# Two graph-attention layers on 64 graphs: rows of exponentials turned in VectorE's 32x32 squares and written in 128-byte pieces, and each output stored right behind its last addition

## The chip, the cores and the metric

The kernel runs on one core of a Trainium2 chip. The metric is the device time of one execution in microseconds. Three executions took 3341.45, 3341.65 and 3340.55 us; the median is 3341.45 us.

## The reference

There are 64 independent graphs of N = 256 nodes with D = 512 features, and a 0/1 adjacency matrix for each. Each graph goes through two residual layers, and everything is float32.

```python
# layer 0: GAT with two attention stages
h = maximum(layernorm(x), 0)
#   stage 1: 4 heads of 256, softmax over sources, concat, bias, elu
#   stage 2: 1 head of 512, softmax over sources, bias
x = x + gat(adj, h, W1, ..., W2, ...)
# layer 1: attention with 8 heads of 64, softmax over neighbours, relu
h = maximum(layernorm(x), 0)
x = x + attend(h, adj, W_proj, W_att, b_att)

# in each stage, for every head:
e    = leaky_relu(a_src[i] + a_dst[j], 0.2)
e    = where(mask, e, -big)
attn = softmax(e)
out  = attn @ xl
```

The kernel avoids the exponential of a 256x256 matrix per head. exp(leaky_relu(s + d)) is the larger of exp(s)exp(d) and exp(0.2 s)exp(0.2 d). Divided by exp(d), which cancels in the softmax, it is the larger of exp(s) and exp(0.2 s) times exp(-0.8 d). So only three vectors of exponentials are needed for a head: two that lie along partitions (one number for each row), and one, exp(-0.8 d), that must lie along the free dimension and be the same on all 128 partitions. Bringing that last vector from "one number per partition" to "a row on every partition" is what most of the change is about.

## The kernel before, in words

A graph's 256 nodes are T = 2 tiles of P = 128 partitions; a node's number is t*128 + q. The three attention stages are called 1, 2 and 3. Every graph goes through steps named as methods of `Graph`: `load`, `stats1` and `norm1` (layer norm), `away1` and `turn1` (the transpose of the normed features, by way of DRAM), the products `m1a`, `m1b` (with W1), `m2` (W2) and `m3` (W_proj), each of them made of seven part products `p1` to `p7` and `c22` with TensorE, `kept` copies on ScalarE (L60) and additions on VectorE (L253), then `exp1`, `edges1`, `gat1`, `out1`, `elu1` for stage 1, and the same with 2 and 3.

In `exp1`, `exp2` and `exp3` ScalarE computes the three exponentials (L275, L466) into a small tile `exs`, which is taken anew for each graph. `spread` (L230) then brings the third one to rows: a DMA on ScalarE's queue writes it to DRAM as `kept` (L233), in pieces of T floats, 8 bytes, since a partition holds the T values of a head side by side; then DMAs on SyncE's queue read it back, broadcast to all partitions (L238): tiles `bc` of two heads, 2 KB in one piece for each partition, 256 KB in all (1 KB and 128 KB in stage 2, which has one head). The row comes back with t innermost, so ScalarE reads every second float of it. `weigh` (L277) makes one 128x256 block of unnormalised attention: ScalarE multiplies the row by a number of each partition (L280, tile `wy`), VectorE takes the maximum with another number and applies the mask (L281, tile `e`). `gat1` (L382), `gat2` (L434) and `gat3` (L484) multiply by `e` on TensorE; the matmuls also give the sums of the softmax, and `out1` (L390, L392), `out2` and `out3` (L490, L492) divide. `out3` ends with GpSimd's addition to the residual `x2` (L494), and `store` (L501) writes `x2` to the output by SyncE's queue. `range` (L497, L498) takes the largest and smallest exponential of a graph, which at the very end decides whether a general path has to run; with these inputs it does not.

The order of work is written out by hand. The kernel's recording mode is a manual schedule: each engine runs its instructions, and each queue issues its DMAs, in the order in which the steps are called. `head`, `order` and `tail` are strings of steps; `run` calls `order` once for each r from 1 to 63, and a step's first number says which graph it is for, relative to r. So one round of `order` works on up to four graphs at once: stages of graph r+1's first products, graph r's stages 1 and 2, graph r-1's stages 2 and 3, and graph r-2's end of stage 3. Of `order` the places that matter here are

```
... 0 edges1 0, 0 edges1 1, 0 m1b p4, ..., 0 gat1 0 0, ...   (graph r, start of a round)
... -2 out3 1 1, -2 out3 1 0, 0 out1 0 1, ...                (last addition to graph r-2)
... 0 exp2, 1 m1a p6, -2 store, -1 edges3 0, ...             (its store)
... 1 m1a p4, 1 m1b p2, 1 exp1, -1 edges3 6, 1 m1b p6, ...   (end of a round)
```

`exp1` stands at the end of a round, and its rows are first used at the start of the next one.

Buffers: four `bc` tiles of two heads (one of stage 2), three `wy`, nine `e`, four banks of PSUM (`pm`) that the products and all `gat` steps share.

Of the kernel before, what the change touches and what calls it, by code (L numbers as in the profile page):

```python
# [17 lines left out]
P = 128  # L18
SLOPE = 0.2
# [78 lines left out]
def short_path(ctx, tc, flags, x, adj, w1, att_src1, att_dst1, b1, w2, att_src2, att_dst2, b2, w_proj, w_att,  # L98
               b_att, out):

    nc = tc.nc
    B, N, D = x.shape
    H1, F1 = att_src1.shape
    HF = H1 * F1
    D2 = w2.shape[1]
    H3 = w_att.shape[0]
    K3 = w_att.shape[1] // 2
    T = N // P
    DC = D // P
    HC = HF // P  # L110
    G = 4
# [26 lines left out]

    ends = const.tile([P, 2, B], F32, name="ends")

    L1, L2, L3 = 4, 1, 2 * G
# [84 lines left out]

    def spread(w, heads):  # L230

        kept = dram.tile([heads, P, T], F32, name=f"kept{heads}")
        nc.scalar.dma_start(kept.rearrange("h p t -> p h t"), w)  # L233
        rows = []
        for h in range(0, heads, 2):
            k = min(2, heads)
            bc = work.tile([P, k, P, T], F32, name=f"bc{k}", bufs=3 * k - 2)
            nc.sync.dma_start(bc.rearrange("p h q t -> p (h q t)"), rows_of(kept[h:h + k], k * N))  # L238
            rows += [bc[:, i].rearrange("p q t -> p t q") for i in range(k)]
        return rows  # L240

    def spread_at_once(w, heads, h):

        pm = ps_mm.tile([P, 512], F32, name="pm")
        for t in range(T):
            nc.tensor.matmul(pm[:, t * P:(t + 1) * P], w[:, h, t:t + 1].to_broadcast([P, P]), ident, start=True, stop=True)
        return pm[:, :N].rearrange("p (t q) -> p t q", t=T)

    def total(dst, pm, add):
        if add is None:  # L250
# [18 lines left out]
        total(lg3[:, t, half, :], pm[:, :L3], add if add is None else add[:, :L3])  # L269
        total(xl3[:, t, half * G:(half + 1) * G, :K3], heads(pm), add if add is None else heads(add))  # L270

    def exps(ex, n, a, o):

        for i, of, by in ((2, o, SLOPE - 1.0), (0, a, 1.0), (1, a, SLOPE)):
            nc.scalar.activation(ex(slice(i * n, (i + 1) * n)), of, AF.Exp, scale=by)  # L275

    def weigh(dst, bc, xw, yw, mask, op):  # L277

        wy = work.tile([P, T, P], F32, name="wy", bufs=3)
        nc.scalar.activation(wy, bc, AF.Copy, scale=yw)  # L280
        nc.vector.scalar_tensor_tensor(dst, wy.rearrange("p t q -> p (t q)"), xw, mask, ALU.max, op)  # L281

    class Graph:

# [29 lines left out]
        def stats1(self):  # L314
            n = Norm()
            for t in range(T):
                n.part(self.xs, t)
            self.ro = n.end()

            exs = self.exs = small.tile([P, 6 * (H1 + 1 + H3)], F32, name="exs")  # L320
            self.ex1 = exs[:, :6 * H1].rearrange("p (i t) -> p i t", t=T)
            self.ex2 = exs[:, 6 * H1:6 * (H1 + 1)].rearrange("p (i t) -> p i t", t=T)
            self.ex3 = exs[:, 6 * (H1 + 1):].rearrange("p (i h t) -> p i h t", i=3, t=T)

        def norm1(self):
            self.h = norm(self.xs, *self.ro)
# [37 lines left out]


        def exp1(self):
            exps(lambda sl: self.ex1[:, sl].rearrange("p h t -> p t h"), H1, xl1[:, :, 0, :L1], xl1[:, :, 1, :L1])
            self.bc1 = spread(self.ex1[:, 2 * H1:], H1)
            self.zt = [work.tile([P, HF], F32, name=f"z{t}", bufs=1) for t in range(T)]

        def edges1(self, h):
            e = self.e[1, h] = work.tile([P, T, N], F32, name="e", bufs=9)
# [40 lines left out]
                left(self.a2, HC // 2)  # L413

        def exp2(self):
            exps(lambda sl: self.ex2[:, sl].rearrange("p h t -> p t h"), 1, xl2[:, :, 0, :L2], xl2[:, :, 1, :L2])
            self.bc2 = None if self.b == B - 1 else spread(self.ex2[:, 2:3], 1)

        def edges2(self):
            e = self.e[2] = work.tile([P, T, N], F32, name="e", bufs=9)  # L420
            bc = self.bc2[0] if self.bc2 else spread_at_once(self.ex2[:, 2:3], 1, 0)
            for s in range(T):
                weigh(e[:, s, :], bc, self.ex2[:, 0, s:s + 1], self.ex2[:, 1, s:s + 1],
                      self.mask[:, s, :], ALU.mult)
# [36 lines left out]
        def exp3(self):  # L461
            nc.vector.tensor_tensor(lg3[:, :, :, :G], lg3[:, :, :, :G],
                                    batt_sb.rearrange("p (a h) -> p a h", a=2)[:, None].to_broadcast([P, T, 2, G]),
                                    ALU.add)
            for i, at, by in ((2, G, SLOPE - 1.0), (0, 0, 1.0), (1, 0, SLOPE)):
                nc.scalar.activation(self.ex3[:, i].rearrange("p (a h) t -> p t a h", a=2), lg3[:, :, :, at:at + G],  # L466
                                     AF.Exp, scale=by)
            self.bc3 = None if self.b == B - 1 else spread(self.ex3[:, 2], H3)

        def edges3(self, h):  # L470
            e = self.e[3, h] = work.tile([P, T, N], F32, name="e", bufs=9)
            bc = self.bc3[h] if self.bc3 else spread_at_once(self.ex3[:, 2], H3, h)
            for s in range(T):
                weigh(e[:, s, :], bc, self.ex3[:, 0, h, s:s + 1], self.ex3[:, 1, h, s:s + 1],
                      self.cap[:, s, :], ALU.min)
# [74 lines left out]
    class Weights:  # L550
# [56 lines left out]
        sums2 0, w sums2 1, 0 exp1, w sums2 2, 0 caps, w sums2 3, 0 edges1 1, 0 edges1 0, 0 edges1 3, 0  # L607
        cap3, 0 edges1 2, 0 gat1 0 0, 0 out1 0 0, 0 gat1 0 1, 0 out1 0 1, 0 gat1 1 0, 0 elu1 0 0, 0 out1 1
        0, 0 elu1 0 1, w load3, 0 gat1 1 1, 1 load, 0 out1 1 1, w dots3 7, 1 stats1, 0 turn2 0 0, 0 elu1 1
        0, 1 masks, 0 turn2 0 1, 0 elu1 1 1, 1 norm1, w dots3 1, 0 m2 p1, w dots3 2, w dots3 0, w dots3 6, 1  # L610
        away1, 0 turn2 1 0, 0 turn2 1 1, w dots3 5, w dots3 4, w dots3 3, 1 turn1, 0 m2 p6, w sums3 0, 0 m2
        p2, w sums3 1, w sums3 2, 0 m2 p7, 0 m2 p4, 0 m2 p5, 1 m1a p1, 1 m1a p6, 0 m2 c22, 1 m1a p5, 0 m2
        p3, 0 exp2, 1 m1a p7, 1 m1a c22, 1 m1b p1, w sums3 3, 1 m1a p4, 1 m1a p3, 1 m1a p2, 1 exp1, 1 bias,
        1 m1b p6, 1 m1b p2, 1 m1b p5, 1 caps
    """
    order = """
        -2 edges3 7, -2 gat3 0 0, -2 edges3 5, -2 gat3 0 1, -1 edges2, 0 m1b p7, -2 out3 0 1, -2 out3 0 0,
        -1 gat2 0, 0 m1b c22, -1 out2 0, -1 stats3 0, 0 m1b p3, -1 gat2 1, 0 edges1 0, 0 edges1 1, 0 m1b p4,
        -1 out2 1, 0 cap3, 1 load, 0 gat1 0 0, 0 edges1 2, 0 edges1 3, 0 out1 0 0, -2 gat3 1 1, -2 gat3 1 0,
        -1 stats3 1, 0 gat1 0 1, -1 norm3, -2 out3 1 1, -2 out3 1 0, 0 out1 0 1, 0 elu1 0 0, 0 elu1 0 1, 0  # L620
        gat1 1 0, -1 turn3, 0 out1 1 0, 0 gat1 1 1, 0 out1 1 1, 1 stats1, -1 m3 p1, 0 turn2 0 0, 0 turn2 0
        1, 0 elu1 1 1, 0 elu1 1 0, -1 m3 p2, -1 m3 p5, 1 masks, 1 norm1, -1 m3 p6, 0 m2 p1, 0 turn2 1 0, 0
        turn2 1 1, 1 away1, -1 m3 p7, 1 bias, -1 m3 c22, 0 m2 p2, -1 m3 p4, -2 range, -1 m3 p3, -1 exp3, 1
        turn1, 0 m2 p6, 0 m2 p5, 0 m2 p7, 1 caps, 1 m1a p1, 0 m2 c22, 0 m2 p3, 0 m2 p4, 0 exp2, 1 m1a p6, -2
        store, -1 edges3 0, -1 edges3 1, 1 m1b p1, 1 m1a p7, 1 m1a p5, 1 m1a c22, -1 edges3 2, 1 m1a p2, -1
        edges3 4, 1 m1a p3, -1 edges3 3, 1 m1a p4, 1 m1b p2, 1 exp1, -1 edges3 6, 1 m1b p6, 1 m1b p5
    """
    tail = """
        -2 range, 0 m1b p5, 0 m1a p2, -1 edges2, -2 gat3 0 0, 0 m1a c22, 0 m1b p6, -2 gat3 0 1, -2 out3 0 1,
        0 m1b p2, -2 edges3 5, -1 gat2 0, 0 exp1, 0 m1a p4, -1 out2 0, -1 stats3 0, -2 edges3 7, -1 gat2 1,  # L630
        -2 gat3 1 0, -1 out2 1, -1 stats3 1, -1 norm3, -2 out3 0 0, -2 gat3 1 1, -2 out3 1 1, -1 turn3, -1
        m3 p1, -1 m3 p2, -1 m3 p5, -1 m3 p6, -1 m3 p7, -1 m3 c22, -2 out3 1 0, -1 m3 p4, -1 m3 p3, -1 exp3,
        -1 range, -1 edges3 1, -1 edges3 4, -1 edges3 0, -1 edges3 3, -1 edges3 2, -1 edges3 5, -1 edges3 7,
        -1 edges3 6, -1 gat3 0 0, -1 gat3 0 1, -2 store, -1 gat3 1 1, -1 out3 0 1, -1 out3 1 1, -1 gat3 1 0,
        -1 out3 0 0, -1 out3 1 0, -1 store
    """
    weights = Weights()

# [293 lines left out]
```

## Time and profile before

| | |
|---|---|
| median of three timed executions | 3341.45 us |
| profiled execution | 3281.43 us |
| its span, first to last instruction | 3279.7 us |
| mean granted TensorE clock | 0.993 |
| TensorE matmul busy | 3155.8 us (96%) |
| VectorE, ScalarE, GpSimd busy | 2267.6, 1959.6, 1178.3 us |
| DMA | 279.19 MB, mean 85 GB/s |
| `wy`, L280, 1646 x | 524 ns each, 746.9 us |
| ScalarE waiting for `bc` ahead of it | 199.4 us in 54 waits |

The profiled execution is one execution, recorded by the hardware's profiler, and here it is 60 us shorter than the timed ones. A row "A <- B: total, times, longest" in a list of waits says that engine A stood idle ahead of the named work until B was done. In a timeline a line gives the start in us from the beginning of the span, the duration, the engine or its queue ("SPq", "ACTq"), the line of the kernel, the operation, and how many are merged; for a DMA the duration is that of its issue, not of the transfer.

### The profile page before, as it was taken

The numbers are of one execution on the slowest core, as the hardware profiler recorded it, in microseconds if no ns is written. First come the engines' busy times: TensorE is split into PE (matmuls) and PEld (weight loads), VectorE is DVE, ScalarE is ACT, GpSimd is POOL, SyncE is SP. The second block draws the span as 40 slices with busy tenths as digits, with TensorE's granted clock in tenths as the row PEclk, the third lists the DMA queues.
The fourth block names the chain that finished last, engine by engine and source line by source line (L and its number), as shares of the span: only waits on it lengthen the run. The fifth ranks groups of instructions, "written<-read, shape, count | busy, mean of one in ns | idle before, by whom it ended". The sixth has DMA issues, their size and how long they took to land. (4 is left out here: it accounts for less than half of the span.)

```text
span 3279.7 us, 60652 instructions
## 1 busy us (share of the span) xinstructions
PE 3155.8 (96%) x21808; PEld 2663.1 (81%) x21808; DVE 2267.6 (69%) x6189; ACT 1959.6 (60%) x4867; POOL 1178.3 (36%) x1433
## 2 busy tenths in 40 slices
PE   4999999999999999999999999999999999999997
PEld 3788888888888888888888888888888888888886
DVE  7667667667667677676676676676776766766765
ACT  2566566566556566655665565566566556665654
POOL 3243343343343342332433433423333334334332
PEclk8999999999999999999999999999999999999998
DMA  4222333323323333323223223233333233332231
GB/s 140 65 79 83 88 87 85 88 88 78 94 82 84 88 82 91 86 83 89 80 82 91 87 79 88 82 91 86 83 91 86 82 89 81 78 94 87 79 94 34
DMA packets 350751, 279.19 MB, mean 85 GB/s; under 512 B 157936, under 2 KB 252016, under 8 KB 350448
## 3 DMA queue, kind: packets, MB, share of 16 engines
q1 hardware_dynamic: 240688, 272.31, 28.3%
q10 hardware_dynamic: 109760, 2.95, 1.9%
q8 instruction: 177, 2.90, 0.4%
q14 instruction: 126, 1.03, 0.2%
HBM read 199.36 MB, written 67.43 MB: 81 GB/s over the span
## 5 line engine op out<-in xcount | busy, mean ns | idle before, releaser
L280 ACT ACTIVATE wy<-bc,exs 128x256 f32<-128x256 f32 x1646 | 746.9, 524 | 263.8 <-DMA bc<-kept 199.4
L281 DVE SCALAR_TENSOR_TENSOR e<-wy,exs,cap 128x256 f32<-128x256 f32 x1024 | 452.2, 483 | 223.0 <-ACT wy L280 223.0
L382 PE MATMUL pm<-xl,e 128*128 128x257 f32 x2048 | 500.3, 387 | 57.5 <-DVE e L281 21.7
L253 DVE TENSOR_TENSOR xl<-pm,kept 128x256 f32<-128x256 f32 (+2 forms) x768 | 321.8, 419 | 282.7 <-PE pm L54 196.9
L494 POOL TENSOR_TENSOR x<-x,o 128x256 f32<-128x256 f32 x256 | 181.0, 728 | 930.9 <-DVE r L490 884.2
L54 PE MATMUL sum<-w_sb,h1s 128*128 128x257 f32 x2048 | 489.0, 381 | 9.3 <-POOL h1s L213 7.0
L382 PEld LDWEIGHTS pm<-xl,e 128*128 128x128 f32 x2048 | 365.5, 190 | 151.4 <-DVE e L281 36.5
L60 ACT ACTIVATE kept<-sum 128x264 f32<-128x264 f32 (+3 forms) x768 | 276.7, 376 | 310.7 <-PE sum L54 294.3
L54 PEld LDWEIGHTS sum<-w_sb,h1s 128*128 128x128 f32 x2048 | 389.4, 190 | 68.7 <-POOL h1s L213 7.2
L54 PE MATMUL pm<-w_sb,h1s 128*128 128x257 f32 x1536 | 370.7, 383 | 10.4 <-DVE xl L253 7.1
L178 POOL TENSOR_TENSOR rstd<-ve,neg_half 128x2 f32<-128x2 f32 x128 | 117.6, 919 | 683.5 <-DVE ve L176 683.5
L54 PEld LDWEIGHTS pm<-w_sb,h1s 128*128 128x128 f32 x1536 | 286.7, 190 | 74.7 <-POOL hs L213 20.7
L281 DVE SCALAR_TENSOR_TENSOR e<-wy,exs,mask 128x256 f32<-128x256 f32 x640 | 276.0, 482 | 65.9 <-ACT wy L280 65.6
L484 PEld LDWEIGHTS pm<-xl,e 128*64 128x64 f32 x8192 | 251.8, 138 | 45.2 <-DVE e L281 23.3
L54 PE MATMUL sum<-w1a_sb,hs 128*128 128x260 f32 x1024 | 269.8, 386 | 11.7 <-DVE w1a_sb L520 4.1
L54 PE MATMUL sum<-w1b_sb,hs 128*128 128x256 f32 x1024 | 271.7, 388 | 4.1 <-ACT hs L343 1.9
L484 PE MATMUL pm<-xl,e 128*64 128x65 f32 x8192 | 270.4, 224 | 1.9 <-DVE e L281 1.2
L54 PE MATMUL sum<-wp_sb,hs 128*128 128x264 f32 x1024 | 271.0, 387 | 1.1 <-ACT kept L60 1.1
L395 ACT ACTIVATE ez<-z 128x512 f32<-128x512 f32 x256 | 159.8, 624 | 181.6 <-DVE z L392 181.6
L392 DVE SCALAR_TENSOR_TENSOR z<-pm,r,b_sb 128x256 f32<-128x256 f32 x512 | 247.8, 484 | 18.3
L434 PE MATMUL pm<-xl,e 128*128 128x257 f32 (+1 forms) x1024 | 243.8, 381 | 1.2 <-DVE e L281 1.2
L54 PEld LDWEIGHTS sum<-w1a_sb,hs 128*128 128x128 f32 x1024 | 190.7, 190 | 51.1 <-issue 13.2
(97 smaller groups left out, 4962.9 us busy)
## 6 DMA issues: line engine op xcount, KB each, us to landing
bc<-kept SPq DMA_DIRECT2D x380, 256.0 KB
xs<-in_x_dram SPq DMA_DIRECT2D x64, 512.0 KB
out_dram<-x SPq DMA_DIRECT2D x64, 512.0 KB
kept_h<-h SPq DMA_DIRECT2D x63, 512.0 KB
h<-kept_h SPq DMA_DIRECT2D x63, 512.0 KB
ad<-in_adj_dram SPq DMA_DIRECT2D x64, 256.0 KB
bc<-kept SPq DMA_DIRECT2D x63, 128.0 KB
w_sb<-in_L_gnn_W_dram SPq DMA_DIRECT2D x4, 512.0 KB
```

Of the source, the lines that this page charges most:

```text
L54: self.nc.tensor.matmul(to[:, :self.n], self.lhs[:, i, c, :], self.rhs[:, i, c, :], start=(first and c == 0), stop=(last and c == self.nk ...
L60: self.nc.scalar.activation(s[:, :self.n], self.sum[:, :self.n], AF.Copy)
L178: nc.gpsimd.tensor_tensor(rstd, ve[:, 0, :], neg_half, ALU.pow)
L253: nc.vector.tensor_tensor(dst, pm, add, ALU.add)
L280: nc.scalar.activation(wy, bc, AF.Copy, scale=yw)
L281: nc.vector.scalar_tensor_tensor(dst, wy.rearrange("p t q -> p (t q)"), xw, mask, ALU.max, op)
L382: nc.tensor.matmul(pm[:, :Q + 1], self.e[1, h][:, s, t * P:(t + 1) * P], xl1[:, s, h, L1:], start=(s == 0), stop=(s == T - 1))
L392: nc.vector.scalar_tensor_tensor(z[:, sl], pm[:, :Q], r, b1_sb[:, sl], ALU.mult, ALU.add)
L395: nc.scalar.activation(ez, z[:, 2 * g * F1:2 * (g + 1) * F1], AF.Relu, scale=-1.0)
L434: nc.tensor.matmul(pm[:, :n], self.e[2][:, s, t * P:(t + 1) * P], xl2[:, s, half, L2:L2 + n], start=(s == 0), stop=(s == T - 1))
L484: nc.tensor.matmul(pv[q:q + 64, h, :], self.e[3, a * G + h][:, s, t * P + q:t * P + q + 64], xl3[:, s, a * G + h, :], start=(s == 0), stop ...
L494: nc.gpsimd.tensor_tensor(to, to, o.rearrange("p h k -> p (h k)"), ALU.add)
```

## The change

1. **Square tiles.** The exponentials of the third kind are written into the first 96 columns of one fixed tile `exs_sb`, 32 columns for each stage, four graphs deep; it is set to 1.0 once at the start. `range` now reduces all 148 columns of a graph instead of 78.
2. **A turn on VectorE.** `spread` transposes a stage's 128x32 block in VectorE's 32x32 squares into a tile `wt`. Partition 32j + c then holds column c (head and t) of the nodes 32j to 32j + 31.
3. **The write.** `wt` goes to DRAM by SyncE's queue instead of ScalarE's: 128 pieces of 128 bytes, the same 16 KB for each stage, used columns or not.
4. **The read.** A row comes back as [j, head and t, i]: four pieces of 512 bytes for each partition and two heads (256 bytes in stage 2), where it was one of 2 KB. ScalarE reads runs of 32 floats instead of every second one.
5. **Steps.** `exp1`, `exp2`, `exp3` are split: `rows1`, `rows2`, `rows3` hold `spread` and stand right behind them.
6. **The store.** In `order`, `-2 store` moves from behind `exp2` to right behind `-2 out3 1 0`.

```diff
+    exs_sb = const.tile([P, 4, 96 + 4 * (H1 + 1 + H3)], F32, name="exs_sb")
+    nc.gpsimd.memset(exs_sb, 1.0)
...
     def spread(w, heads):
-        kept = dram.tile([heads, P, T], F32, name=f"kept{heads}")
-        nc.scalar.dma_start(kept.rearrange("h p t -> p h t"), w)
+        wt = small.tile([P, 32], F32, name="wt")
+        nc.vector.transpose(wt, w)
+        kept = dram.tile([4, 32, 32], F32, name=f"kept{heads}")
+        nc.sync.dma_start(kept.rearrange("j c i -> (j c) i"), wt)
         rows = []
         for h in range(0, heads, 2):
             k = min(2, heads)
-            bc = work.tile([P, k, P, T], F32, name=f"bc{k}", bufs=3 * k - 2)
-            nc.sync.dma_start(bc.rearrange("p h q t -> p (h q t)"), rows_of(kept[h:h + k], k * N))
-            rows += [bc[:, i].rearrange("p q t -> p t q") for i in range(k)]
+            bc = work.tile([P, 4, T * k, 32], F32, name=f"bc{k}", bufs=3 * k - 2)
+            nc.sync.dma_start(bc.rearrange("p j c i -> p j (c i)"),
+                              kept[:, T * h:T * (h + k), :].rearrange("j c i -> j (c i)")[None].to_broadcast([P, 4, 32 * T * k]))
+            rows += [bc[:, :, T * i:T * (i + 1), :].rearrange("p j t i -> p t j i") for i in range(k)]
...
-    def exps(ex, n, a, o):
-        for i, of, by in ((2, o, SLOPE - 1.0), (0, a, 1.0), (1, a, SLOPE)):
-            nc.scalar.activation(ex(slice(i * n, (i + 1) * n)), of, AF.Exp, scale=by)
+    def exps(w, ex, n, a, o):
+        for to, of, by in ((w[:, :n * T].rearrange("p (h t) -> p t h", t=T), o, SLOPE - 1.0),
+                           (ex[:, :n].rearrange("p h t -> p t h"), a, 1.0),
+                           (ex[:, n:].rearrange("p h t -> p t h"), a, SLOPE)):
+            nc.scalar.activation(to, of, AF.Exp, scale=by)
...
     def weigh(dst, bc, xw, yw, mask, op):
-        wy = work.tile([P, T, P], F32, name="wy", bufs=3)
-        nc.scalar.activation(wy, bc, AF.Copy, scale=yw)
-        nc.vector.scalar_tensor_tensor(dst, wy.rearrange("p t q -> p (t q)"), xw, mask, ALU.max, op)
+        wy = work.tile([P, N], F32, name="wy", bufs=3)
+        nc.scalar.activation(wy.rearrange("p (t j i) -> p t j i", t=T, j=4), bc, AF.Copy, scale=yw)
+        nc.vector.scalar_tensor_tensor(dst, wy, xw, mask, ALU.max, op)
...
+            exs = self.exs = exs_sb[:, self.b % 4]
...
         def exp1(self):
-            exps(lambda sl: self.ex1[:, sl].rearrange("p h t -> p t h"), H1, xl1[:, :, 0, :L1], xl1[:, :, 1, :L1])
-            self.bc1 = spread(self.ex1[:, 2 * H1:], H1)
+            exps(self.w[0], self.ex1, H1, xl1[:, :, 0, :L1], xl1[:, :, 1, :L1])
...
+        def rows1(self):
+            self.bc1 = spread(self.w[0], H1)
...
     order:
-        ... -2 out3 1 1, -2 out3 1 0, 0 out1 0 1, ... 0 exp2, 1 m1a p6, -2 store, -1 edges3 0, ...
+        ... -2 out3 1 1, -2 out3 1 0, -2 store, 0 out1 0 1, ... 0 exp2, 0 rows2, 1 m1a p6, -1 edges3 0, ...
-        ... -1 m3 p3, -1 exp3, 1 turn1, ... 1 m1b p2, 1 exp1, -1 edges3 6, ...
+        ... -1 m3 p3, -1 exp3, -1 rows3, 1 turn1, ... 1 m1b p2, 1 exp1, 1 rows1, -1 edges3 6, ...
```

The last graph still takes its rows of stages 2 and 3 from TensorE (`spread_at_once`), with the new layout. `head` and `tail` get the `rows` steps too; their stores stay where they are.

More of the change, by code (lines that the diff above doesn't have):

```diff
@@ L236, in spread, with spread_at_once @@
             k = min(2, heads)
-            bc = work.tile([P, k, P, T], F32, name=f"bc{k}", bufs=3 * k - 2)
-            nc.sync.dma_start(bc.rearrange("p h q t -> p (h q t)"), rows_of(kept[h:h + k], k * N))
-            rows += [bc[:, i].rearrange("p q t -> p t q") for i in range(k)]
+            bc = work.tile([P, 4, T * k, 32], F32, name=f"bc{k}", bufs=3 * k - 2)
+            nc.sync.dma_start(bc.rearrange("p j c i -> p j (c i)"),
+                              kept[:, T * h:T * (h + k), :].rearrange("j c i -> j (c i)")[None].to_broadcast([P, 4, 32 * T * k]))
+            rows += [bc[:, :, T * i:T * (i + 1), :].rearrange("p j t i -> p t j i") for i in range(k)]
         return rows
-    def spread_at_once(w, heads, h):
+    def spread_at_once(w, h):
         pm = ps_mm.tile([P, 512], F32, name="pm")
@@ L246, in spread_at_once @@
             nc.tensor.matmul(pm[:, t * P:(t + 1) * P], w[:, h, t:t + 1].to_broadcast([P, P]), ident, start=True, stop=True)
-        return pm[:, :N].rearrange("p (t q) -> p t q", t=T)
+        return pm[:, :N].rearrange("p (t j i) -> p t j i", t=T, j=4)
     def total(dst, pm, add):
@@ L318, in stats1 @@
             self.ro = n.end()
[L320 to L323, printed above, removed]
+            exs = self.exs = exs_sb[:, self.b % 4]
+            self.ex1 = exs[:, 96:96 + 4 * H1].rearrange("p (i t) -> p i t", t=T)
+            self.ex2 = exs[:, 96 + 4 * H1:100 + 4 * H1].rearrange("p (i t) -> p i t", t=T)
+            self.ex3 = exs[:, 100 + 4 * H1:].rearrange("p (i h t) -> p i h t", i=2, t=T)
+            self.w = [exs[:, 32 * l:32 * (l + 1)] for l in range(3)]
         def norm1(self):
@@ L415, in exp2, with rows2 @@
         def exp2(self):
-            exps(lambda sl: self.ex2[:, sl].rearrange("p h t -> p t h"), 1, xl2[:, :, 0, :L2], xl2[:, :, 1, :L2])
-            self.bc2 = None if self.b == B - 1 else spread(self.ex2[:, 2:3], 1)
+            exps(self.w[1], self.ex2, 1, xl2[:, :, 0, :L2], xl2[:, :, 1, :L2])
+        def rows2(self):
+            self.bc2 = None if self.b == B - 1 else spread(self.w[1], 1)
         def edges2(self):
             e = self.e[2] = work.tile([P, T, N], F32, name="e", bufs=9)
-            bc = self.bc2[0] if self.bc2 else spread_at_once(self.ex2[:, 2:3], 1, 0)
+            bc = self.bc2[0] if self.bc2 else spread_at_once(self.w[1][:, :T].rearrange("p (h t) -> p h t", t=T), 0)
             for s in range(T):
@@ L464, in exp3, with rows3 @@
                                     ALU.add)
[L465 to L468, printed above, removed]
+            self.w3 = self.w[2][:, :H3 * T].rearrange("p (h t) -> p h t", t=T)
+            for to, at, by in ((self.w3, G, SLOPE - 1.0), (self.ex3[:, 0], 0, 1.0), (self.ex3[:, 1], 0, SLOPE)):
+                nc.scalar.activation(to.rearrange("p (a h) t -> p t a h", a=2), lg3[:, :, :, at:at + G], AF.Exp, scale=by)
+        def rows3(self):
+            self.bc3 = None if self.b == B - 1 else spread(self.w[2], H3)
         def edges3(self, h):
             e = self.e[3, h] = work.tile([P, T, N], F32, name="e", bufs=9)
-            bc = self.bc3[h] if self.bc3 else spread_at_once(self.ex3[:, 2], H3, h)
+            bc = self.bc3[h] if self.bc3 else spread_at_once(self.w3, h)
             for s in range(T):
@@ L606, in short_path @@
         5, 0 m1a p2, 0 m1a c22, w dots2 1, 0 m1a p3, w dots2 6, 0 m1a p4, w dots2 4, w columns2, 0 m1b p3, w
[L607 to L614, printed above, removed]
+        sums2 0, w sums2 1, 0 exp1, 0 rows1, w sums2 2, 0 caps, w sums2 3, 0 edges1 1, 0 edges1 0, 0 edges1
+        3, 0 cap3, 0 edges1 2, 0 gat1 0 0, 0 out1 0 0, 0 gat1 0 1, 0 out1 0 1, 0 gat1 1 0, 0 elu1 0 0, 0
+        out1 1 0, 0 elu1 0 1, w load3, 0 gat1 1 1, 1 load, 0 out1 1 1, w dots3 7, 1 stats1, 0 turn2 0 0, 0
+        elu1 1 0, 1 masks, 0 turn2 0 1, 0 elu1 1 1, 1 norm1, w dots3 1, 0 m2 p1, w dots3 2, w dots3 0, w
+        dots3 6, 1 away1, 0 turn2 1 0, 0 turn2 1 1, w dots3 5, w dots3 4, w dots3 3, 1 turn1, 0 m2 p6, w
+        sums3 0, 0 m2 p2, w sums3 1, w sums3 2, 0 m2 p7, 0 m2 p4, 0 m2 p5, 1 m1a p1, 1 m1a p6, 0 m2 c22, 1
+        m1a p5, 0 m2 p3, 0 exp2, 0 rows2, 1 m1a p7, 1 m1a c22, 1 m1b p1, w sums3 3, 1 m1a p4, 1 m1a p3, 1
+        m1a p2, 1 exp1, 1 rows1, 1 bias, 1 m1b p6, 1 m1b p2, 1 m1b p5, 1 caps
     """
@@ L619, in short_path @@
         -1 out2 1, 0 cap3, 1 load, 0 gat1 0 0, 0 edges1 2, 0 edges1 3, 0 out1 0 0, -2 gat3 1 1, -2 gat3 1 0,
[L620 to L626, printed above, removed]
+        -1 stats3 1, 0 gat1 0 1, -1 norm3, -2 out3 1 1, -2 out3 1 0, -2 store, 0 out1 0 1, 0 elu1 0 0, 0
+        elu1 0 1, 0 gat1 1 0, -1 turn3, 0 out1 1 0, 0 gat1 1 1, 0 out1 1 1, 1 stats1, -1 m3 p1, 0 turn2 0 0,
+        0 turn2 0 1, 0 elu1 1 1, 0 elu1 1 0, -1 m3 p2, -1 m3 p5, 1 masks, 1 norm1, -1 m3 p6, 0 m2 p1, 0
+        turn2 1 0, 0 turn2 1 1, 1 away1, -1 m3 p7, 1 bias, -1 m3 c22, 0 m2 p2, -1 m3 p4, -2 range, -1 m3 p3,
+        -1 exp3, -1 rows3, 1 turn1, 0 m2 p6, 0 m2 p5, 0 m2 p7, 1 caps, 1 m1a p1, 0 m2 c22, 0 m2 p3, 0 m2 p4,
+        0 exp2, 0 rows2, 1 m1a p6, -1 edges3 0, -1 edges3 1, 1 m1b p1, 1 m1a p7, 1 m1a p5, 1 m1a c22, -1
+        edges3 2, 1 m1a p2, -1 edges3 4, 1 m1a p3, -1 edges3 3, 1 m1a p4, 1 m1b p2, 1 exp1, 1 rows1, -1
+        edges3 6, 1 m1b p6, 1 m1b p5
     """
@@ L629, in short_path @@
         -2 range, 0 m1b p5, 0 m1a p2, -1 edges2, -2 gat3 0 0, 0 m1a c22, 0 m1b p6, -2 gat3 0 1, -2 out3 0 1,
[L630 to L635, printed above, removed]
+        0 m1b p2, -2 edges3 5, -1 gat2 0, 0 exp1, 0 rows1, 0 m1a p4, -1 out2 0, -1 stats3 0, -2 edges3 7, -1
+        gat2 1, -2 gat3 1 0, -1 out2 1, -1 stats3 1, -1 norm3, -2 out3 0 0, -2 gat3 1 1, -2 out3 1 1, -1
+        turn3, -1 m3 p1, -1 m3 p2, -1 m3 p5, -1 m3 p6, -1 m3 p7, -1 m3 c22, -2 out3 1 0, -1 m3 p4, -1 m3 p3,
+        -1 exp3, -1 rows3, -1 range, -1 edges3 1, -1 edges3 4, -1 edges3 0, -1 edges3 3, -1 edges3 2, -1
+        edges3 5, -1 edges3 7, -1 edges3 6, -1 gat3 0 0, -1 gat3 0 1, -2 store, -1 gat3 1 1, -1 out3 0 1, -1
+        out3 1 1, -1 gat3 1 0, -1 out3 0 0, -1 out3 1 0, -1 store
     """
```

## The prediction

> **What bounds the kernel now.** I read the page first, then TensorE's list of waits over the steady part, then two single rounds of the loop, then SyncE's and ScalarE's timelines in one round. The page:
>
> ```profile
> span 3279.7 us, 60652 instructions
> ...
> PE 3155.8 (96%) x21808; PEld 2663.1 (81%) x21808; DVE 2267.6 (69%) x6189; ACT 1959.6 (60%) x4867; POOL 1178.3 (36%) x1433
> ...
> PEclk8999999999999999999999999999999999999998
> ```
>
> TensorE is busy 96% of the span at an almost full granted clock. No edit here removes matmul work, so what can be won is TensorE's idle time, about 124 us. Some of it belongs to the start. The list of waits, TensorE only, from 177.8 to 3170.7 us (60 rounds; columns: total us, how often, longest):
>
> ```profile
> PE pm L382 <- DVE r L390: 20.5, 47, 0.5
> PE pm L382 <- DVE r L490: 13.2, 52, 0.3
> PE pm L382 <- DVE e L281: 12.1, 21, 1.2
> PE pm L54 <- DVE xl L253: 6.1, 40, 0.2
> PE sum L54 <- ACT kept L60: 2.7, 8, 0.5
> ```
>
> The first three rows are 45.8 us, 0.76 us a round, and all lie in `gat1`, the first layer's aggregation (L382). Everything else in that stretch adds 11 us. So 57 us is about the ceiling in steady state. To see what causes the three rows, I compared a bad round (1572.8 to 1625.2) with a good one (477.5 to 524.9). The bad round's list of waits has these rows for TensorE and ScalarE:
>
> ```profile
> PE pm L382 <- DVE e L281: 1.1, 1, 1.1
> PE pm L382 <- DVE r L390: 0.5, 1, 0.5
> PE pm L382 <- DVE r L490: 0.3, 1, 0.3
> ...
> ACT wy L280 <- DMA bc<-kept: 4.7, 1, 4.7
> ```
>
> The good round has no TensorE wait at all, and the last row is only:
>
> ```profile
> ACT wy L280 <- DMA bc<-kept: 2.5, 1, 2.5
> ```
>
> So ScalarE stands waiting for the rows of layer 1's exponentials (`bc`), `edges1` comes late, then VectorE catches up late, and TensorE waits for data (L281) and then for banks of PSUM that VectorE has not emptied (L390, L490). About 2.5 us of ScalarE's wait is free; beyond it TensorE loses roughly what is added. Why the rows are late stands in SyncE's and ScalarE's queue timelines of the next bad round (start us, duration us):
>
> ```profile
> 1639.43 0.39 SPq L501 DMA_DIRECT2D out_dram<-x  x1
> ...
> 1642.22 0.37 ACTq L233 DMA_DIRECT2D kept<-exs  x1
> ...
> 1648.70 0.79 SPq L238 DMA_DIRECT2D bc<-kept  x2
> ...
> 1652.31 0.94 ACT L280 ACTIVATE wy<-bc,exs 128x256 f32<-128x256 f32 x2 [4.56 <-DMA bc<-kept]
> ```
>
> `exp1` writes its exponentials to DRAM at 1642.22. The broadcast read can start only at 1648.70, 6.48 us later, and ScalarE gets it at 1652.31, 3.61 us after that. The 512 KB store of the output is issued 2.8 us ahead of the small write. The same write of the first graph, at the start where no store is in flight, shows the difference:
>
> ```profile
> 44.36 0.38 ACTq L233 DMA_DIRECT2D kept<-exs  x1
> ...
> 47.40 0.82 SPq L238 DMA_DIRECT2D bc<-kept  x2
> ```
>
> There it takes 3.04 us, with the same 512 pieces of 8 bytes. So 3.4 us of the 6.48 is what lies in front of it, most likely the store, and not the size of the pieces. The good round (494.72 to 499.46) takes 4.74 us.
>
> **What the Trainium skill says.** "DMA: Bandwidth & Descriptors", section "Issuing engines are not separate DMA queues": DMAs of all issuing engines run on the same 16 DMA engines and interleave. The 6.48 against 3.04 us agrees: the write was on ScalarE's queue, the store on SyncE's. The same page's Specifications put the smallest transfer for line rate at 512 B, with read-modify-write below. New row pieces are 512 B (256 B in layer 2), so they sit at that edge; the trace has 512 B pieces in `kept_h<-h`, below. "VectorE: DVE Perf Modes", section "The three transpose paths": VectorE transposes only 32x32 blocks, 311 ns for 128x128 bf16. No run here has that shape; the trace's own row (L206) is used. "SBUF — State Buffer", section "Door 1: The DMA port swizzle": lines of 16 bytes, full rate from two hits a line. `wy` now reads every second float, two hits a line, so making it contiguous should win little. The trace agrees as far as it goes: reading every fourth float (L333) took 1297 ns where the contiguous L186 took 807.
>
> **The change, part by part.** Sums are made against the profiled execution, 3281.43 us for a span of 3279.7. The timed median is 3341.45, 60 us above, and no view shows why. I carry a saving over from one to the other as microseconds.
>
> Store moved: it goes from SyncE's queue ahead of `exp1`'s write to about 1662, right after POOL's last two L494 additions (end at 1661.8 in that round). On SyncE it comes after the loads of the next graph (1654.9, 1655.4) and ahead of `kept_h` (1671). It waits for POOL well under a round and 9 us pass before SyncE has anything else, so nothing queues behind it. Its landing must not touch `kept_h`; with 9 us it should be done. Gain: the small write falls from 6.48 to 3.0 us in a bad round, from 4.74 to 3.0 in a good one.
>
> Write in 128-byte pieces, moved to SyncE: 16 KB in 128 pieces instead of 512 pieces of 8 B. Layer 2's write has just 128 pieces (1636.04 to 1639.01) and takes 2.97 us, no better than 3.04 for 512. So the pieces themselves win nothing here; layer 3's (1024 pieces, 1627.19 to 1631.39) may win 1.2 us, where its rows have slack, needed at 1636.7. I take 3.0 us for all three. ScalarE loses 190 issues of 0.37 us from its queue; the trace charges it only 0.2 us a round for that ("issue").
>
> VectorE's transposes, 190 new ones of 128x32. L206 (128x512) takes 1134 ns, about 2.1 ns an element over a floor near 0.1 to 0.16 (L390, one element, 159 ns): 0.16 to 0.23 us, I take 0.2. That is 0.6 us a round on an engine idle for 30%. Where each stands: layer 3's waits for an exponential of 0.2 us behind L462, but VectorE then sat 1.34 us waiting for `h<-kept_h`, which hides both; if that load came early it costs 0.4 us of VectorE. Layer 2's falls into VectorE's 3.04 us wait for `wy` at 1637. Layer 1's stands behind `m1b p2`'s addition, which ends at 1643.0 where ScalarE issued at 1642.22: the write now starts at about 1643.27, 1.05 us later. Behind it waits only `edges3 6`, which waited 0.2 us for ScalarE anyway.
>
> SyncE: `kept` waits on the queue where its `bc` waited already, with nothing between, so no new queueing.
>
> Rows read in four pieces: 512 instead of 128 per 256 KB. Each DMA engine carries 32 rather than 8 a tile. `kept_h<-h` wrote 64 pieces of 512 B per engine in 3.24 us in a quick round (2668.09 to 2671.33), 4.71 in a slow one; less 2.97 for a small write, that is 4 to 27 ns a piece. For 24 more pieces: 0.1 to 0.65 us; I take 0.3. Below nothing is excluded, as the bytes are the same.
>
> The reductions of `range` go from 78 to 148 elements, some 70 ns each and two a round; VectorE idles there for a microsecond. The memset is one POOL instruction at the start, ahead of an 11 us wait. `wy` may get up to 56 ns shorter (524 against 468 for the PSUM form); I count 0.
>
> Sum for layer 1's rows, bad round: -6.48 + 1.05 + 3.0 + 0.3 = 2.1 us earlier, ScalarE's wait 4.6 to 2.5. Good round: -4.74 + 4.35 = 0.4 earlier, 2.5 to 2.1. That is the region where TensorE's `gat1` waits vanish. I keep 0.1 us a round of the 0.76, so 0.66 x 63 = 42 us, plus 1 to 2 for the last round, whose chain runs through this write (6.16 us) and its rows. Say 43: 3279.7 to 3237 for the span, 3341.45 to **3298** for the median.
>
> **Rivals.** (1) The forecast, 0.55; its own range, 3283 to 3312, holds 0 to 0.3 us of wait kept and some of the other rows gone. (2) The 60 us between profile and median are this very wait. If every round of a timed run is as bad as the worst (1.9 us of TensorE wait, against a mean of 0.95), that alone is 60 us. Then up to 63 x 1.7 = 107 us goes: 3234. For it: the size fits. Against: nothing shows the timed rounds. 0.15. (3) Half the gain, 3320: rows in four pieces land 1 us later than I take, or something other than the store (rows of layers 2 and 3, just issued) delays the write. 0.14. (4) No change, 3340: the small write stays at 5 to 6 us and the 1.05 us of later start eats the rest; against it, the first graph's 3.04. 0.07. (5) Slower: pieces of the broadcast rows cost far more than written ones. From 100 ns a piece (24 x 100 = 2.4 us) layer 1's gain is gone, and above it layer 3's four tiles pile up, 3.2 us each, in the stretch where ScalarE has no slack; at 150 ns, 2.4 us a round more, about 3341 + 75 = 3415. Against: 27 ns is the most that the trace allows for a written piece. 0.09.
>
> **The numbers.** A measurement tells about 0.2%, 7 us, from no change. Faster: cases 1, 2 and 3, and a little of 4: 0.86. Same: most of 4, 0.05. Slower: 0.09. The range leaves out case 5 and the ends of 2 and 4: 3235 to 3335.
>
> **What would show it.** In the new profile the write of layer 1 to its `bc` should be about 3 us, ScalarE's wait for `bc` fall from 199 us in total to 100 to 150, L382's waits for L390, L490 and L281 to under 10 us, and TensorE's busy time stay near 3156 with its share at 97%. A transpose row of about 0.2 us should stand in VectorE's list with no TensorE wait on it. If `bc` lands over 4.5 us after its issue, step "rows in four pieces" was wrong; if the write still takes 5 us, the store was not the cause. It would be wrong as a whole if TensorE's waits fall as said and the median does not follow.

## The result and the profile after

The changed kernel takes 3215.99 us (median of four, 3214.73 to 3218.9) against 3341.55 us for the kernel before beside it: a ratio of 0.9626, 95% interval 0.9609 to 0.9643, so 126 us or 3.7% faster. The forecast was 3298 with a range of 3235 to 3335. The sign was right, the size was a third.

The profile of the changed kernel (its page):

```profile
span 3217.2 us, 60904 instructions
...
PE 3133.7 (97%) x21808; PEld 2670.7 (83%) x21808; DVE 2282.5 (71%) x6379; ACT 1917.4 (60%) x4867; POOL 1179.1 (37%) x1434
```

Its profiled execution (3218.9 us) agrees with its timed ones. That of the kernel before had been 60 us shorter than its timed ones; this gap turned out to be the key. TensorE's list of waits, changed kernel, 177.8 to 3110 us:

```profile
PE pm L54 <- DVE xl L260: 5.5, 36, 0.2
PE sum L54 <- ACT kept L60: 3.0, 9, 0.5
PE pm L394 <- DVE r L402: 1.9, 5, 0.4
PE pm L394 <- DVE r L506: 1.3, 5, 0.3
...
PE pm L394 <- DVE e L290: 0.5, 2, 0.3
```

L394 is the old L382, `gat1`. Its three waits, 45.8 us before, are 3.7 us. The two rows of L54, which were not part of the target, are about what they were. So the aim of the forecast was right: `gat1` no longer waits for layer 1's rows. How the rows get there is in the timeline of one round, here with the lines of VectorE, of SyncE's queue and of ScalarE that matter:

```profile
1615.07 0.20 DVE L237 STREAM_TRANSPOSE wt<-exs_sb 128x32 f32<-128x32 f32 x1
1615.30 0.33 SPq L239 DMA_DIRECT2D kept<-wt  x1
...
1617.45 0.91 SPq L244 DMA_DIRECT2D bc<-kept  x2
...
1623.11 1.71 ACT L289 ACTIVATE wy<-bc,exs_sb 128x256 f32<-128x256 f32 x4 [3.19 <-DMA bc<-kept]
```

The write takes 2.15 us here, where the round shown of the kernel before took 6.48. The read takes 5.66 us, where it took 3.61: the layout in DRAM that made the write short made the read long. ScalarE still waits 3.19 us, and TensorE waits for no `e` of these blocks. The page's list of DMA issues has the medians from issue to landing (last number, in us), for the tiles of layers 1 and 3 together and for the writes of all three layers:

```profile
bc<-kept SPq DMA_DIRECT2D x380, 256.0 KB, 5.7
...
kept<-wt SPq DMA_DIRECT2D x190, 16.0 KB, 1.4
```

### The profile page after: what moved, and what is told of

Read it like the earlier page. It is cut to its first block, busy times and chain, and to the rows that moved or that the text cites. A ratio compares the mean times of both kernels' runs of the same rounds, so it can differ in the third digit from the quotient of the medians.

```text
span 3217.2 us, 60904 instructions
## 1 busy us (share of the span) xinstructions
PE 3133.7 (97%) x21808; PEld 2670.7 (83%) x21808; DVE 2282.5 (71%) x6379; ACT 1917.4 (60%) x4867; POOL 1179.1 (37%) x1434
## 5 line engine op out<-in xcount | busy, mean ns | idle before, releaser
L289 ACT ACTIVATE wy<-bc,exs_sb 128x256 f32<-128x256 f32 x1646 | 706.9, 498 | 176.1 <-DMA bc<-kept 129.3
L394 PE MATMUL pm<-xl,e 128*128 128x257 f32 x2048 | 489.9, 386 | 17.6 <-DVE e L290 13.6
L290 DVE SCALAR_TENSOR_TENSOR e<-wy,exs_sb,cap 128x256 f32<-128x256 f32 x1024 | 435.8, 478 | 92.4 <-ACT wy L289 92.4
L54 PE MATMUL sum<-w_sb,h1s 128*128 128x257 f32 x2048 | 489.0, 381 | 9.3 <-POOL h1s L216 7.0
L54 PEld LDWEIGHTS sum<-w_sb,h1s 128*128 128x128 f32 x2048 | 389.3, 190 | 68.7 <-POOL h1s L216 7.2
L394 PEld LDWEIGHTS pm<-xl,e 128*128 128x128 f32 x2048 | 374.3, 190 | 84.0 <-DVE e L290 14.9
L54 PE MATMUL pm<-w_sb,h1s 128*128 128x257 f32 x1536 | 371.1, 383 | 10.4 <-DVE xl L260 6.5
L54 PEld LDWEIGHTS pm<-w_sb,h1s 128*128 128x128 f32 x1536 | 287.0, 190 | 74.9 <-POOL hs L216 20.1
L54 PE MATMUL sum<-w1a_sb,hs 128*128 128x260 f32 x1024 | 269.6, 386 | 11.7 <-ACT kept L60 4.5
L290 DVE SCALAR_TENSOR_TENSOR e<-wy,exs_sb,mask 128x256 f32<-128x256 f32 x640 | 270.3, 480 | 13.1 <-ACT wy L289 12.8
L54 PE MATMUL sum<-w1b_sb,hs 128*128 128x256 f32 x1024 | 271.9, 388 | 2.9 <-ACT hs L353 1.5
L54 PE MATMUL sum<-wp_sb,hs 128*128 128x264 f32 x1024 | 270.8, 387 | 1.3 <-ACT kept L60 1.1
L54 PEld LDWEIGHTS sum<-w1a_sb,hs 128*128 128x128 f32 x1024 | 191.4, 190 | 50.2 <-issue 15.2
```

What stands on the lines that cost most here:

```text
L54: self.nc.tensor.matmul(to[:, :self.n], self.lhs[:, i, c, :], self.rhs[:, i, c, :], start=(first and c == 0), stop=(last and c == self.nk ...
L289: nc.scalar.activation(wy.rearrange("p (t j i) -> p t j i", t=T, j=4), bc, AF.Copy, scale=yw)
L290: nc.vector.scalar_tensor_tensor(dst, wy, xw, mask, ALU.max, op)
L394: nc.tensor.matmul(pm[:, :Q + 1], self.e[1, h][:, s, t * P:(t + 1) * P], xl1[:, s, h, L1:], start=(s == 0), stop=(s == T - 1))
```

## The experiments

Below, "the small write" is layer 1's `kept`, from its issue to the issue of its `bc`, and "the read" goes from there to ScalarE's first `wy` on it. Medians are those of the traces: of the small write over all 64 graphs, of the read over the graphs for which ScalarE waited.

### The kernel before, profiled again

No edit. It asks what the 60 us between its profile and its times are.

> The kernel before, unchanged, profiled a second time, to see whether the 60 us between its profiled execution (3281) and its timed ones (3341) are a property of the kernel. If the waits for the rows differ from execution to execution (theory: the timed ones have every round as bad as the worst), this profile shows a span nearer 3341 and waits of TensorE in gat1 of 90 to 110 us in place of 46. If the gap is something outside these waits, the profile shows 46 us again and the gap stays. Time: 3341 in both.

Measured: 3344.87 us, ratio 0.9996 (0.9985 to 1.0007). The profiled execution took 3345.02 us with a span of 3343.3 us, so here profile and times agree. TensorE's list of waits (177.8 to 3080 us) and the page's line:

```profile
PE pm L382 <- DVE e L281: 54.5, 48, 2.3
PE pm L382 <- DVE r L390: 24.9, 52, 0.5
PE pm L382 <- DVE r L490: 13.4, 53, 0.3
```

```profile
PE 3166.7 (95%) x21808; PEld 2661.9 (80%) x21808; DVE 2265.0 (68%) x6189; ACT 1959.2 (59%) x4867; POOL 1179.4 (35%) x1433
```

The three waits are 92.8 us here, twice the 45.5 of the first profile in the same stretch, and ScalarE waits 286.6 us for `bc` instead of 199.4. The median small write is 6.67 us where the first profile has 5.67; the read is the same, 3.57 and 3.50. So the two profiles of one kernel differ in the duration of an 8-byte-piece write and in the waits behind it. That the timed executions of the first session differed from their profile in the same way is the likely reading, but it is not shown: of those executions only the times are known. VectorE also waits 14.8 us in this profile, in 23 waits, for the store to be done before it can write `x` (L444); but behind each of them it waits another 1.8 to 2.4 us for `wy`, so these waits did not end last. A bad round of this profile, SyncE's and ScalarE's queues:

```profile
1672.13 0.39 SPq L501 DMA_DIRECT2D out_dram<-x  x1
...
1682.02 0.79 SPq L238 DMA_DIRECT2D bc<-kept  x2
```

```profile
1675.08 0.37 ACTq L233 DMA_DIRECT2D kept<-exs  x1
...
1685.71 1.77 ACT L280 ACTIVATE wy<-bc,exs 128x256 f32<-128x256 f32 x4 [5.10 <-DMA bc<-kept]
```

Here the write takes 6.94 us.

The idle time of TensorE is the span less its busy time: 176.6 us here and 83.5 in the changed kernel. That is 93.1 of the 126.1 us. The other 33.0 us are in the *busy* time of the same 21808 matmuls. TensorE's timeline of this profile shows how:

```profile
1631.13 1.89 PE L434 MATMUL pm<-xl,e 128*128 128x257 f32 x8
1632.87 1.03 PE L54 MATMUL sum<-w1b_sb,hs 128*128 128x256 f32 x4
1635.50 2.00 PE L382 MATMUL pm<-xl,e 128*128 128x257 f32 x8 [1.61 <-DVE e L281]
1637.44 2.09 PE L484 MATMUL pm<-xl,e 128*64 128x65 f32 x64
1640.01 1.97 PE L382 MATMUL pm<-xl,e 128*128 128x257 f32 x8 [0.48 <-DVE r L390]
1642.23 1.97 PE L382 MATMUL pm<-xl,e 128*128 128x257 f32 x8 [0.25 <-DVE r L490]
```

Without a stop a group starts before the last one ends: 1632.87 against 1631.13 + 1.89 = 1633.02, an overlap of 0.15 us. Behind a stop nothing overlaps, and eight matmuls take 1.97 to 2.00 us where the undisturbed eight take 1.89. So a stop costs some 0.25 us beside what the list of waits calls the wait. By the lists of waits this profile has 153 stops in `gat1` and the changed kernel 12; 141 more stops make 35 us, near the 33. The 0.25 is an estimate from these few lines. The other profiles bear it out: of twelve (the run with the write on SyncE's queue has its stops elsewhere and is left out) a straight line gives 0.22 us of busy time for each stop in `gat1`, and no profile lies more than 7 us off it. Two profiles of the same kernel, without stops in `gat1`, differ by 4 us (3128.6 and 3132.7).

### Either half alone

Only the store moved:

```diff
-        ... 0 exp2, 1 m1a p6, -2 store, -1 edges3 0, ...
+        ... -2 out3 1 1, -2 out3 1 0, -2 store, 0 out1 0 1, ... 0 exp2, 1 m1a p6, -1 edges3 0, ...
```

> Only the store is moved; rows still go in 8-byte pieces from ScalarE's queue and come back in one 2 KB piece. Theory S (the store in front of layer 1's small write makes the rows late): the write takes 3.0 us, ScalarE's wait for bc falls to 60 to 110 us in total, time 3215 to 3240. Theory P (the 8-byte pieces are what makes the write slow): the write still takes 5 to 6 us, time 3320 to 3341.

Measured: 3228.62 us, ratio 0.9646 (0.963 to 0.9662) against 3347.95 of the kernel before beside it. TensorE's waits in `gat1` are 4.2 us in all (1.2 for L390, 3.0 for L490). The small write is still slow, but less (ScalarE's issue; then SyncE's, from a narrow window of its timeline):

```profile
1616.26 0.37 ACTq L233 DMA_DIRECT2D kept<-exs  x1
```

```profile
1619.66 0.80 SPq L238 DMA_DIRECT2D bc<-kept  x2
```

3.40 us here; the median is 4.24.

Only the squares, with the store in its old place:

```diff
# the changed kernel with
-        ... -2 out3 1 0, -2 store, 0 out1 0 1, ... 1 m1a p6, -1 edges3 0, ...
+        ... -2 out3 1 0, 0 out1 0 1, ... 1 m1a p6, -2 store, -1 edges3 0, ...
```

> The squares, the 128-byte pieces and the rows in four pieces, but the store in its old place. Theory S: layer 1's write still takes 5 to 6 us behind the store and starts 1 us later, time 3330 to 3355. Theory P: the write takes 2.2 us as in the changed kernel, time 3216 to 3230.

Measured: 3221.12 us, ratio 0.9618 (0.9602 to 0.9634). The store is again in front of the small write, in SyncE's own queue:

```profile
1614.56 0.44 SPq L517 DMA_DIRECT2D out_dram<-x  x1
1619.55 0.34 SPq L239 DMA_DIRECT2D kept<-wt  x1
1621.81 0.92 SPq L244 DMA_DIRECT2D bc<-kept  x2
```

and the write of 128-byte pieces takes 2.26 us all the same (median 1.62). So each half takes away enough of the lateness by itself, and the moved store adds next to nothing to the squares: 0.9626 and 0.9618, with overlapping intervals.

That 128-byte pieces are quick *beside* the store does not follow. The store is here issued 4.97 us ahead of layer 1's write (median), where it was 2.81 and 2.58 us in the two profiles of the kernel before: layer 2's write got shorter by 1.6 us (1.43 instead of 3.02), so the store, which stands behind layer 2's read on SyncE's queue, is issued earlier, and layer 1's write comes about a microsecond later. The store's row on three pages, with its median time to landing, of the changed kernel, of this run, and of the kernel before in the last session:

```profile
out_dram<-x SPq DMA_DIRECT2D x64, 512.0 KB, 2.8
out_dram<-x SPq DMA_DIRECT2D x64, 512.0 KB, 5.8
out_dram<-x SPq DMA_DIRECT2D x64, 512.0 KB, 7.5
```

So when layer 1's write is issued in this run, the store is nearly through. In all 61 graphs with a store ahead of it the write lands after the store, by 0.16 us or more. For the kernel before, the trace of the last session has the store's landing in 16 graphs: in 13 of them layer 1's read is issued 0.20 to 0.31 us behind it. There the small write ended when the store did, as theory S says. What the squares do with the store in its old place is, at least in part, to let the store be gone earlier. How a write of 128-byte pieces would do 2.8 us behind the store was not tried, and why the store lands so differently in its two places is not shown.

The queue alone, that is the store moved and the 8-byte write on SyncE's queue:

```diff
# only the store moved, and
-        nc.scalar.dma_start(kept.rearrange("h p t -> p h t"), w)
+        nc.sync.dma_start(kept.rearrange("h p t -> p h t"), w)
```

> As the run with only the store moved, but the small write goes by SyncE's queue in the same 8-byte pieces: it tells the queue from the pieces. Both theories: the queue alone does nothing, within 5 us of the run with only the store moved. If ScalarE's queue was what the write waited in, this one is faster by more than that.

Measured: 3245.6 us, ratio 0.9686 (0.9664 to 0.9708): 17 us *slower* than with ScalarE's queue, against both theories. `gat1` waits less than there (1.6 us), but a new wait stands first in TensorE's list (and L54's wait for `kept` grows from 1.9 to 9.8 us), and in VectorE's list there is more of the wait it comes from (82.8 us here, 45.5 with only the store moved):

```profile
PE sum L54 <- DVE hs L206: 15.7, 16, 1.6
```

```profile
DVE hs L206 <- DMA h<-kept_h: 82.8, 52, 4.0
```

Layer 3's write, 1024 pieces of 8 bytes, is now issued on the same queue right behind the load of `h` for the next graph, and `h` comes later: of the loads whose landing the trace has, 16 of 56 took over 4.6 us, and none of 47 with only the store moved. That the one delays the other is argued from the order, not shown. The changed kernel has its write on the same queue, in 128 pieces, and no such wait of TensorE.

### Lateness by itself

If lateness of layer 1's rows is the whole story, then the changed kernel, made late on purpose, must become as slow as the kernel before. `rows1` is put behind two, four or six of VectorE's `e` steps (0.48 us each) without any change in the work:

```diff
# e6, two steps
-  1 exp1, 1 rows1, -1 edges3 6,
+  1 exp1, -1 edges3 6, 1 rows1,
# e8, four steps, at the start of the next round (the head's rows1 goes too)
-  -2 edges3 7, -2 gat3 0 0, -2 edges3 5,
+  -2 edges3 7, 0 rows1, -2 gat3 0 0, -2 edges3 5,
# e7, six steps
+  -2 edges3 7, -2 gat3 0 0, -2 edges3 5, 0 rows1,
```

> The changed kernel with layer 1's turn, write and read behind edges3 6, so two of VectorE's 0.48 us steps later, about 0.9 us. Allowance theory: ScalarE waits about 3.0 us in each round, TensorE loses 0 to 0.4 us a round, 3216 to 3245. If lateness of these rows was not what the change removed: 3216.

> The same, four VectorE steps later, about 1.9 us. Allowance theory: ScalarE waits about 4.0 us, TensorE about 1 us a round and 0.3 in its busy time, 3270 to 3310. If something else made the gain: under 3245.

> The same, behind edges3 6 of one graph and edges3 7 and 5 of another: six VectorE steps later, about 2.8 us. Allowance theory: ScalarE waits about 4.9 us a round, as in the kernel before, TensorE's waits in gat1 come back to 70 to 110 us and its busy time rises by 20 to 35 us (each stop also lays bare the end of the matmul before it), 3310 to 3350. If something else in the change made the gain, the time stays under 3260.

Measured: 3222.08, 3333.14 and 3368.16 us, ratios 0.9743 (0.9724 to 0.9762), 1.0068 (1.005 to 1.0086) and 1.0173 (1.0153 to 1.0192) against a kernel before of 3309.22 in that session. The last one, TensorE's list of waits and the page:

```profile
PE pm L394 <- DVE e L290: 70.4, 56, 2.5
PE pm L394 <- DVE r L402: 22.5, 51, 0.4
PE pm L394 <- DVE r L506: 13.0, 51, 0.3
```

```profile
PE 3171.9 (94%) x21808; PEld 2670.7 (79%) x21808; DVE 2282.0 (68%) x6379; ACT 1915.8 (57%) x4867; POOL 1179.2 (35%) x1434
```

The three rows that the change removed are back, with the store out of the way and the large pieces in place. So it is lateness that costs, whatever makes it. The four-step run overshot what was expected (3270 to 3310), as did the six-step one (3310 to 3350); the two-step one moved the median wait of ScalarE only from 2.1 to 2.5 us, not to 3.0.

### The rows in one piece

```diff
# the changed kernel with
-        kept = dram.tile([4, 32, 32], F32, name=f"kept{heads}")
-        nc.sync.dma_start(kept.rearrange("j c i -> (j c) i"), wt)
+        kept = dram.tile([32, 4, 32], F32, name=f"kept{heads}")
+        nc.sync.dma_start(kept.rearrange("c j i -> j c i"), wt)
...
-            bc = work.tile([P, 4, T * k, 32], F32, ...)
-            (read in four pieces)
+            bc = work.tile([P, T * k, P], F32, name=f"bc{k}", bufs=3 * k - 2)
+            nc.sync.dma_start(bc.rearrange("p c q -> p (c q)"), rows_of(kept[T * h:T * (h + k)], k * N))
+            rows += [bc[:, T * i:T * (i + 1), :].rearrange("p t (j i) -> p t j i", j=4) for i in range(k)]
```

> The changed kernel, but kept is laid out in DRAM so that a head's row is contiguous: the rows come back in one 2 KB piece for each partition again (1 KB in stage 2), and the write stays 128 pieces of 128 bytes. If the four pieces are what made the rows land in 5.2 us where they took 3.6, bc lands 1.6 us earlier and ScalarE's wait for it falls from 129 us in total to under 50. Theory of the free allowance (a wait of ScalarE below about 2.5 us costs nothing): time the same within 6 us, 3208 to 3218. If every microsecond of that wait counts: 60 to 90 us faster, 3130 to 3155.

Measured: 3210.85 us, ratio 0.9703 (0.9688 to 0.9718) against 3309.22. The read is back at 3.54 us in the median, the write a little longer, 1.98 us, and ScalarE's list of waits has

```profile
ACT wy L288 <- DMA bc<-kept: 51.3, 48, 8.0
```

where the changed kernel has 129.3. The 78 us that ScalarE waits less for `bc` are not 78 us of time: the free part of the wait was worth nothing, and most of it changed its name (ScalarE's wait for VectorE's `e` ahead of `wy` grew from 24.9 to 94.3 us). What is left of `gat1`'s waits (3.7 us) is gone.

A last session put three kernels on one chip.

> The kernel before once more, on the chip of the two runs beside it, for the waits that belong to its time there: time and waits of TensorE in gat1 should lie on one line with the two profiles so far (span 3280 with 46 us, 3343 with 93 us).

> The changed kernel on the same chip: 3210 to 3222 whatever the kernel before takes here, since its small write took 1.5 us in all runs so far and does not meet the store.

> The version with the rows in one piece again, on the same chip as the changed kernel: 4 to 9 us faster than it (its waits in gat1 are gone, and with them a few us of busy time).

Measured: the kernel before 3256.44 us (median of the nine runs beside the others; 3249.65 in the profiled execution), the changed kernel 3214.45, ratio 0.9874 (0.9856 to 0.9892), and the version with rows in one piece 3209.66, ratio 0.9861 (0.9843 to 0.9879). That version is 4.8 us ahead of the changed kernel by medians, as expected. The two intervals against the kernel before overlap, but of five runs each only one of the changed kernel (3211.16) lies below the slowest of the other (3211.77). Against the kernel before it is faster in both sessions.

### All profiles together

| run | ScalarE waits for `bc`, us | waits in `gat1`, us | TensorE busy, us | span, us |
|---|---|---|---|---|
| rows in one piece (first) | 51.3 | 0 | 3128.6 | 3205.0 |
| rows in one piece (last session) | 58.7 | 0 | 3132.7 | 3207.1 |
| changed kernel (last session) | 101.2 | 1.6 | 3130.8 | 3211.6 |
| store moved, write on SyncE's queue | 114.2 | 1.6 | 3148.0 | 3248.6 |
| two steps late | 119.7 | 3.7 | 3138.5 | 3219.5 |
| only the squares | 124.5 | 5.3 | 3137.7 | 3220.7 |
| changed kernel (first) | 129.3 | 3.7 | 3133.7 | 3217.2 |
| only the store moved | 134.4 | 4.2 | 3143.1 | 3223.6 |
| before, last session | 157.9 | 22.1 | 3146.8 | 3247.9 |
| before, first profile | 199.4 | 45.5 | 3155.8 | 3279.7 |
| before, second profile | 286.6 | 92.8 | 3166.7 | 3343.3 |
| four steps late | 289.0 | 79.8 | 3166.4 | 3334.1 |
| six steps late | 319.0 | 105.9 | 3171.9 | 3366.5 |

(`gat1`: 177.8 to 3080 us; 3110 for the changed kernel. A window of the same length holds a few more rounds in a fast kernel.) Up to some 135 us of ScalarE's wait, about 2 us a round, little happens: spans of 3205 to 3224 us. From there `gat1`'s waits, the busy time and the span rise together, and a late changed kernel lies close to the kernel before. The one row that stands apart is the write on SyncE's queue, whose waits are not in `gat1`.

## Why the prediction was right and wrong

**The mechanism: right.** The chain from late rows to ScalarE, to VectorE, to `gat1` was read correctly, and the late runs show it by itself. So was the free part of ScalarE's wait: 2.5 us was read from a good round, and the table bends between 2.1 and 2.5 us a round (134 and 158 us).

**"I carry a saving over from one to the other as microseconds": wrong, and it is the largest error.** The sum was made with 0.76 us a round, from an execution whose span was 60 us below the timed median. The second profile, which agrees with its times, has 92.8 us in 57 rounds, 1.6 us a round: there was twice as much to win. The rival (2), that the 60 us are this very wait, fits this profile, with 47 us more wait in `gat1` and 11 us more busy time than in the first one; it had been given 0.15 because no view showed the timed rounds. Its price, 3234, was still 18 us above the result.

**A term that was missing in all cases: the stop itself.** The ceiling of 57 us was read off the list of waits. Each stop costs some 0.22 to 0.25 us more (estimates from the lines and the profiles above), which the profile books as busy; 33 us between the second profile and the changed kernel, 22 us between the first one and it. "TensorE's busy time stay near 3156" was wrong, it fell to 3133.7. With both terms the sum closes: 93.1 of idle time and 33.0 of busy time are 126.1 us, the difference of the spans.

**"So the pieces themselves win nothing here; I take 3.0 us": wrong.** The reading compared 512 pieces with 128 pieces of the same 8 bytes, which says nothing about 128-byte pieces. Layer 2's write has 128 pieces before and after, and went from 3.02 us with 8 bytes each (3.07 when that write goes by SyncE's queue) to 1.43 with 128; layer 1's takes 1.47. The step "what lies in front of it, most likely the store" was right in the main: the store moved alone is worth 0.9646, and in the last session's profile of the kernel before most of the writes ended with the store. But without the store the 8-byte write still takes 4.24 us in the median, not the 3.0 of the first graph.

**"Rows in four pieces ... I take 0.3": wrong by 1.3 us.** The read went from 3.6 to 5.24 us in the median; one piece brought it back to 3.54. The bound of 4 to 27 ns a piece was taken from a write to DRAM of 512-byte pieces, and does not hold for this read: 24 more pieces for each DMA engine took 1.5 to 1.7 us, some 60 to 70 ns a piece. So rival (5), slower from 100 ns a piece, was nearer than the prediction took it to be. (Its own sum slipped too: 2.4 us a round would be 151 us, and the 75 us that it names go with 50 ns above the 100, which is 1.2 us.) The Trainium skill's "DMA: Bandwidth & Descriptors", Specifications, with its 512 B for line rate, does not tell the two apart either; here the measurement decides. That the forecast for the rows' arrival came out close is luck, since the errors of the write and of the read nearly cancel: by the terms of the sum, rows came 0.9 + 1.5 + 5.2 = 7.6 us after ScalarE's old point of issue, where 1.05 + 3.0 + 3.9 = 7.95 was expected.

**Smaller steps: right.** The transposes take 204 ns (0.2 expected) and no engine is charged with a wait for them, though VectorE itself waits 114 us ahead of layer 2's. The write of layer 1 is issued at 1615.30, 1.15 us behind ScalarE's exponentials at 1614.15, against 0.23 before: 0.9 us later (1.05). `range` went from 224 to 297 ns (70 more expected). `wy` became 26 ns shorter, 524 to 498, inside the 0 to 56 that was left open. VectorE's wait for `wy` ahead of layer 3's blocks fell from 223 to 92 us, but mainly because the 114 us ahead of layer 2's transpose now stand in the same place; neither is seen in TensorE's waits. Not foreseen: at the start, layer 1's rows of the first graph are 3.4 us later (ScalarE's first `wy` at 54.80 instead of 51.41), since the transpose stands behind other VectorE work there.

## What to carry to other kernels

A profiled execution that is well below the timed ones is a warning that some wait in it varies: before summing, ask which of the waits could be longer in the others, and profile the unchanged kernel a second time. A list of waits gave a lower bound of what the stops of TensorE cost here, because behind each stop the matmuls no longer overlap with the ones before. And a helper engine's wait is worth something only beyond what the bottleneck leaves free: once it is down to that, every cure that makes the data early enough is worth the same, and cures do not add up.

## What was not expected of the hardware

The duration of the 8-byte-piece write changes from session to session, and with it the kernel before: 3341.55 and 3347.95 us, 3309.22 us, 3256.44 us, the last two on the same chip. Its median small write was 6.67 us in the profile at 3343 us, 5.67 at 3280 and 4.84 at 3248. The changed kernel, with 128-byte pieces, stayed between 3214.45 and 3215.99 us, and its write between 1.47 and 1.50 us in the median of every profile with its layout and its store. So the size of the gain depends on when it is measured: the changed kernel was 3.7% and 1.3% faster than the kernel before beside it. What changes between sessions is open; nothing in these profiles shows it.

A small write did not land before a 512 KB store that had been issued 3.7 to 5.5 us ahead of it: not once in the 61 graphs of the run with only the squares, where both go by SyncE's queue. In the kernel before, where they go by two queues, the read that waits for the write was issued 0.20 to 0.31 us behind the store's landing in 13 of 16 graphs. The store itself took 2.8 us in its new place and 5.8 to 7.5 us behind layer 2's read (medians).

A broadcast read of 256 KB in pieces of 512 bytes took 5.09 us in the median where pieces of 2 KB took 3.59, on the same chip in the last session.
